# Graph network with attention on one core: the value matrix applied after the weighted sums, and a short last set of chunks

## The chip, the cores and the metric

The kernel runs on one core of one Trainium2 chip. The metric is the device time of one execution in microseconds (us). Engines are named as in the profile: PE (TensorE matmuls), PEld (the loading of matmul weights, which the same engine does), DVE (VectorE), ACT (ScalarE), POOL (GpSimd) and SP (SyncE). POOL and SP have only DMA work and register work in the parts that matter here.

## The reference

There are 6250 nodes with 256 features and 106250 edges, sorted by destination; every node has an edge to itself, so a node has 17 edges in the mean. Two blocks follow each other.

```
h = relu(layernorm(x))
for l in 0, 1, 2:                                    # relational layers, 8 edge types
    msg = (h @ W_rel[l][type])[src]                  # one matrix for each type
    h   = relu(segment_sum(msg, dst) + h @ W_root[l] + bias[l])
x1 = x + h
g  = relu(layernorm(x1))
v  = g @ Wv + bv ;  q = v @ wq + bq ;  k = v @ wk + bk
e  = leaky_relu(q[src] + k[dst], 0.2)
a  = softmax of e over the edges of each dst
out = x1 + segment_sum(a * v[src], dst)
```

## The kernel before, in words

Edges are taken in 831 chunks of 128. Consecutive chunks form sets: 47 sets of 15 chunks and then 9 of 14, 56 in all. A set covers at most 128 consecutive destination nodes, beginning at the destination of its first edge; where the next set begins with the same node, the last chunk of a set is also given to the next one ("ahead"). `node_ranges` gives, for each chunk position in a set, the range of nodes that it can touch. If the input does not fit these ranges, a second, general program runs; it does not run here.

The program has a preparation (edges turned, positions checked, first layernorm, table `tab[0]` written), three layers and the attention phase.

In a layer (`order` loop), each chunk costs one indirect DMA from POOL (L717) that fetches 128 rows of the layer's table, three bf16 parts of each feature row, into `msg` (36 buffers). PE multiplies them (L896) with a 0/1 matrix `hot` that DVE makes (L864) and that separates nodes and edge types. Sums gather in PSUM `bank`s and are copied by ACT to `ag` (`evacuate`, L772). What follows for a set is `finish`, a generator that is advanced by one step after each chunk of the next set: a transposition of the set's own rows (`pt`, L782), 18 f32 matmuls of 256 columns with the weights (L797, L801; each is two PE records) spread over 12 steps, the bias (L805), a split into three bf16 parts and a write to the next table. With its last `yield` that makes 14 steps; the call that finds the generator at its end uses one call more. In the third layer the 18 matmuls take 8 steps, and five steps come after them: residual and write to `xa`, layernorm (L822), two transpositions (L827) with relu (L829), two matmuls with `Wv` (L833), and the bias, the heads q and k (L842) and the write of rows of 257 numbers (v and q) to `hx`. What is left of `finish` after a layer's last chunk runs then. The order of this part is written out by hand (`manual_schedule`), and each engine takes its instructions in that order. SP loads a set's first node and its own rows at chunk 4.

The first gather of a layer reads a table that the layer before has written to its last row.

In the attention phase each chunk is one indirect DMA of 257-number rows of `hx` (48 buffers, `head`). DVE makes a mask (L961), ACT adds q (L968), PE transposes (L970, three PSUM buffers `pq`), ACT and DVE form the logits and their maxima (L973 to L981), ACT takes the exponential of the whole set (L983), PE transposes back (L988, three PSUM buffers `pe`), ACT and DVE copy to `ex` (L991, L993), and PE adds up `ex` times the rows (L995, one f32 matmul of 256 columns for each chunk, two records) into `po`. DVE scales and adds x1 (L1001). Here a planner orders the instructions of each engine when the kernel is built, with program order as priority; each engine takes them in that fixed order.

Of the kernel before, what the change touches and what calls it, by code (L numbers as in the profile page):

```python
# [19 lines left out]
P = 128  # L20
# [6 lines left out]
CW = 15  # L27
SPREAD = 4.5
# [7 lines left out]
def node_ranges(n: int, mean: float) -> list[tuple[int, int]]:  # L36


    wander = math.sqrt(mean - 1.0) / mean**1.5
    out = []  # L40
    for k in range(n):
        a, b = P * k, P * (k + 1) - 1
        lo = math.floor(a / mean - SPREAD * wander * math.sqrt(a) - 1)
        hi = math.ceil(b / mean + SPREAD * wander * math.sqrt(b) + 2)
        out.append((max(lo, 0) if k else 0, min(hi, P) if k < n - 1 else P))
    return out
# [383 lines left out]
def kernel(  # L430
# [28 lines left out]
    NW = -(-NC // CW)  # L459
    NLONG = NC - NW * (CW - 1)  # L460
    NS = NW - NLONG
    CL = NLONG * CW
    sizes = [CW] * NLONG + [CW - 1] * NS
    first_c = [sum(sizes[:t]) for t in range(NW)]
    ranges = {n: node_ranges(n, E / N) for n in (CW, CW - 1)}
# [31 lines left out]
    def by_window(a: bass.AP):  # L497

        return ((slice(0, NLONG), a[:, :CL].rearrange("p (t k) -> p t k", k=CW), CW),
                (slice(NLONG, NW), a[:, CL:NC].rearrange("p (t k) -> p t k", k=CW - 1), CW - 1))  # L500

    with tc.tile_pool(name="prep", bufs=1) as prep, \
# [49 lines left out]
        for at, view, k in by_window(dst_t):  # L552
            nc.vector.tensor_copy(base[:, at], view[0:1, :, 0])
        nc.vector.tensor_copy(front[:, 1:NLONG + 1],
                              dst_t[0:1, CW - 1:CL:CW])
        nc.vector.tensor_copy(front[:, NLONG + 1:NW],
                              dst_t[0:1, CL + CW - 2:NC - (CW - 1):CW - 1])
# [12 lines left out]
        for n in (CW, CW - 1):  # L570
# [19 lines left out]
        for to, of, b in ((loc_p, dst_t, base_b), (seg_p, seg_t, seg_b)):  # L590
            nc.vector.memset(to[:, 0:1], -1.0)
            nc.vector.tensor_tensor(to[:, 1:NLONG + 1], of[:, CW - 1:CL:CW],
                                    b[:, 1:NLONG + 1], ALU.subtract)
            nc.vector.tensor_tensor(to[:, NLONG + 1:NW], of[:, CL + CW - 2:NC - (CW - 1):CW - 1],
                                    b[:, NLONG + 1:NW], ALU.subtract)
# [4 lines left out]
        viol = prep.tile([P, 8], F32)  # L600
# [15 lines left out]


# [10 lines left out]
        nc.vector.tensor_scalar(ends[:, 2:3], base[:, NW - 1:NW], -1.0, float(N - P) - 0.5,  # L628
# [28 lines left out]
    def statistics(pool, xt: bass.AP, n: int):  # L657
        mv = pool.tile([P, 4, 2], F32, name="mv")
        for i in range(n):
            st = pool.tile([P, 6], F32, name="st")  # L660
            nc.vector.bn_stats(st, xt[:, i, :])
            nc.vector.bn_aggr(mv[:, i, :], st)
        rstd = pool.tile([P, 4], F32, name="rstd")
        nc.scalar.activation(rstd[:, :n], mv[:, :n, 1], AF.Sqrt, bias=eps)
        nc.vector.reciprocal(rstd[:, :n], rstd[:, :n])
# [39 lines left out]
    def ordered_path():  # L705
# [7 lines left out]
        k_n = cst.tile([P, NW], F32)  # L713
        bs = path.enter_context(tc.tile_pool(name="bs", bufs=3))
# [14 lines left out]
        with ExitStack() as s:  # L729
# [12 lines left out]
            wv_s = one.tile([P, KH, D], F32)  # L742
            bv_s = one.tile([P, D], F32)
            wq_s = one.tile([P, D], F32)
            wk_s = one.tile([P, D], F32)
            bq_s = one.tile([P, 1], F32)
            bk_s = one.tile([P, 1], F32)
# [14 lines left out]
            def load_head():  # L762
                nc.scalar.dma_start(wv_s, wv.rearrange("(k p) e -> p k e", p=P))
                for to, of in ((bv_s, bv), (wq_s, wq), (wk_s, wk)):
                    nc.scalar.dma_start(to, rows_bcast(of, D))
                for to, of in ((bq_s, bq), (bk_s, bk)):
                    nc.scalar.dma_start(to, rows_bcast(of, 1))

            def evacuate(banks, half: int, ag: bass.AP):

                for h in range(KH):
                    nc.scalar.copy(ag[:, h, :, half * (P // 2):(half + 1) * (P // 2)],  # L772
                                   banks[half][h].rearrange("p (n r) -> p r n", r=R))

            def finish(l: int, at, xt: bass.AP, ag: bass.AP, weights, t: int):


                wr, wo, bb = weights
                pt = ops.tile([P, KH, P], F32, name="pt")
                for k in range(KH):  # L780
                    for i in range(3):
                        nc.tensor.matmul(pt[:, k, :], xt[:, i, k * P:(k + 1) * P], ident_b,  # L782
                                         start=(k == 0 and i == 0), stop=(k == KH - 1 and i == 2),
                                         skip_group_check=True)
                x_t = rp.tile([P, KH, P], F32, name="x_t")
                nc.scalar.copy(x_t, pt)
                yield
                last = l + 1 == L
                parts = STEPS - (6 if last else 2)
# [3 lines left out]
                for i in range(parts):  # L793
                    upto = len(todo) * (i + 1) // parts
                    for r, h in todo[done:upto]:
                        if r < R:
                            nc.tensor.matmul(po, ag[:, h, r, :], wr[:, h, r, :],  # L797
                                             start=(r == 0 and h == 0), stop=False,
                                             skip_group_check=True)
                        else:  # L800
                            nc.tensor.matmul(po, x_t[:, h, :], wo[:, h, :], start=False,  # L801
# [3 lines left out]
                nc.vector.tensor_add(po, po, bb)  # L805
                if not last:
                    hml = rp.tile([P, 3, D], BF16, name="hml")
                    split(hml, po, po, "relu")
                    nc.sync.dma_start(tab[l + 1][ds(at, P), :], hml.rearrange("p s d -> p (s d)"))
                    yield  # L810
                    return
                x0 = rp.tile([P, D], F32, name="x0")
                if t < NW - 1:
                    nc.sync.dma_start(x0, x[ds(at, P), :])
                else:
                    gather(x0, x, last_c)
                x1 = rp.tile([P, 1, D], F32, name="x1")
                nc.vector.scalar_tensor_tensor(x1[:, 0, :], po, 0.0, x0, op0=ALU.max, op1=ALU.add)
                nc.sync.dma_start(xa[ds(at, P), :], x1[:, 0, :])
                yield  # L820
                mv, rstd = statistics(rp, x1, 1)
# [224 lines left out]
```

## Time and profile before

| | us |
|---|---|
| median of three runs (lowest, highest) | 4529.12 (4519.02, 4529.94) |
| the profiled execution | 4520.3 |
| its span, first to last instruction | 4518.4 |
| first gather of layers 1, 2, 3 and of attention | 120.66, 1189.70, 2256.10, 3411.92 |
| last gather of layers 1, 2, 3 and of attention | 1158.45, 2227.32, 3331.59, 4457.52 |

| share of the span | PE | PEld | DVE | ACT | POOL |
|---|---|---|---|---|---|
| busy | 84% | 69% | 45% | 26% | 70% |

A line of a timeline gives start, duration, engine, source line, operation, output and inputs, how many instructions are drawn together, and in brackets how long the engine had been idle and what ended that. A group of instructions gives busy time (overlaps counted once), mean ns of one, and idle time before. A line of the chain of waits gives who waited for whom, the total, how often, and the longest. In a table by stretches the columns are busy us and number of instructions for PE, PEld, DVE, ACT and POOL, then granted PE clock, DMA share and GB/s.

### The profile page before, as it was taken

The numbers are of one execution on the slowest core, as the hardware profiler recorded it, in microseconds if no ns is written. First come the engines' busy times: TensorE is split into PE (matmuls) and PEld (weight loads), VectorE is DVE, ScalarE is ACT, GpSimd is POOL, SyncE is SP. The second block draws the span as 40 slices with busy tenths as digits, with TensorE's granted clock in tenths as the row PEclk, the third lists the DMA queues.
The fourth block names the chain that finished last, engine by engine and source line by source line (L and its number), as shares of the span: only waits on it lengthen the run. The fifth ranks groups of instructions, "written<-read, shape, count | busy, mean of one in ns | idle before, by whom it ended". The sixth has DMA issues, their size and how long they took to land. (4 is left out here: it accounts for less than half of the span.)

```text
span 4518.4 us, 81585 instructions
## 1 busy us (share of the span) xinstructions
PE 3775.3 (84%) x29932; PEld 3129.4 (69%) x29932; DVE 2030.9 (45%) x5907; ACT 1179.9 (26%) x2622; POOL 3177.1 (70%) x3411
## 2 busy tenths in 40 slices
PE   0799999999899999999888989999985777777776
PEld 0677777777677777777677777777774666555555
DVE  6333333333233333333334444444444666666664
ACT  3111111111111111111111111111114555555554
POOL 2777777777577777777577777777636777777773
PEclk5899999999899999999999999999996877778888
DMA  4666666666566666666566666666633444444442
GB/s 152 214 179 180 179 180 179 179 179 181 154 180 180 179 180 180 179 180 180 149 182 186 188 186 186 178 177 179 176 107 96 120 119 119 120 121 120 117 119 60
DMA packets 305210, 722.81 MB, mean 160 GB/s; under 512 B 63179, under 2 KB 158487, under 8 KB 304800
## 3 DMA queue, kind: packets, MB, share of 16 engines
q0 software_dynamic: 199536, 599.93, 47.2%
q1 hardware_dynamic: 94940, 108.40, 7.3%
q10 hardware_dynamic: 10324, 9.18, 0.6%
q8 instruction: 237, 3.88, 0.4%
q14 instruction: 173, 1.42, 0.1%
HBM read 663.43 MB, written 53.87 MB: 159 GB/s over the span
## 5 line engine op out<-in xcount | busy, mean ns | idle before, releaser
L717 POOL DMA_INDIRECT msg<-tab,src_t x2493 | 2357.4, 946 | 855.0 <-issue 398.1
L896 PE MATMUL bank<-hot,msg 128*128 128x104 bf16 (+16 forms) x17982 | 1738.8, 240 | 288.2 <-DMA msg<-tab,src_t 175.1
L896 PEld LDWEIGHTS <-msg 128*128 128x128 bf16 x18972 | 1397.8, 98 | 687.2 <-DMA msg<-tab,src_t 311.2
L797 PE MATMUL po<-wr,ag 128*128 128x256 f32 x5376 | 1494.9, 392 | 6.7 <-DVE hml L655 4.9
L864 DVE TENSOR_SCALAR hot<-up,seg 128x104 bf16<-128x104 f32 (+10 forms) x2493 | 953.0, 430 | 647.4 <-PE bank L896 643.1
L717 POOL DMA_INDIRECT head<-hx,src_t x831 | 785.5, 945 | 306.8 <-issue 138.2
L797 PEld LDWEIGHTS po<-wr,ag 128*128 128x128 f32 x5376 | 898.0, 191 | 66.8 <-DVE hml L655 6.2
L772 ACT COPY ag<-bank 128x512 f32<-128x512 f32 x672 | 361.6, 591 | 1915.7 <-PE bank L896 1903.7
L805 DVE TENSOR_TENSOR po<-po,bb 128x256 f32<-128x256 f32 x168 | 72.6, 432 | 1061.7 <-PE po L801 1026.2
L995 PE MATMUL po<-head,ex 128*128 128x256 f32 x1772 | 451.4, 412 | 1.6 <-DVE ex L993 0.5
L995 PEld LDWEIGHTS po<-head,ex 128*128 128x128 f32 x1772 | 363.8, 211 | 68.0 <-ACT ex L991 14.2
L970 PE MATMUL pq<-ident,qm 128*128 128x128 f32 x886 | 202.0, 320 | 171.1 <-ACT qm L968 169.9
L968 ACT ACTIVATE qm<-other,head 128x128 f32<-128x128 f32 x886 | 299.5, 397 | 146.1 <-issue 117.7
L988 PE MATMUL pe<-ident,c 128*128 128x128 f32 x886 | 190.4, 388 | 134.5 <-ACT c L983 134.5
L974 DVE TENSOR_REDUCE tops<-pq 128x1 f32<-128x512 f32 x224 | 152.4, 680 | 323.4 <-ACT c L973 323.1
L970 PEld LDWEIGHTS pq<-ident,qm 128*128 128x128 f32 x886 | 126.0, 153 | 233.2 <-ACT qm L968 218.7
L988 PEld LDWEIGHTS pe<-ident,c 128*128 128x128 f32 x886 | 162.2, 205 | 154.4 <-ACT c L983 148.7
L961 DVE TENSOR_SCALAR other<-up,loc 128x128 f32<-128x128 f32 x831 | 256.6, 340 | 10.4 <-ACT qm L968 10.4
L801 PE MATMUL po<-wo,x_t 128*128 128x256 f32 x672 | 173.2, 380 | 0.0
L652 ACT ACTIVATE hml<-po 128x256 bf16<-128x256 f32 x112 | 43.0, 384 | 489.1 <-DVE po L805 398.5
L975 DVE SCALAR_TENSOR_TENSOR c<-pq,k_n,c 128x512 f32<-128x512 f32 x224 | 164.7, 735 | 0.0
L991 ACT COPY ex<-pe 128x512 f32<-128x512 f32 x112 | 64.5, 576 | 352.4 <-PE pe L988 352.4
(135 smaller groups left out, 1588.7 us busy)
## 6 DMA issues: line engine op xcount, KB each, us to landing
msg<-tab,src_t POOLq DMA_INDIRECT x2493
xt<-tab SPq DMA_DIRECT2D x168, 192.0 KB
tab<-hml SPq DMA_DIRECT2D x112, 192.0 KB
head<-hx,src_t POOLq DMA_INDIRECT x831
tab<-hml SPq DMA_DIRECT2D x12, 768.0 KB
hx<-row SPq DMA_DIRECT2D x56, 128.5 KB
xa<-x SPq DMA_DIRECT2D x56, 128.0 KB
xt<-xa SPq DMA_DIRECT2D x56, 128.0 KB
```

What stands on the lines that cost most here:

```text
L717: nc.gpsimd.indirect_dma_start(out=to, out_offset=None, in_=table[:N, :], in_offset=bass.IndirectOffsetOnAxis(ap=index, axis=0))
L772: nc.scalar.copy(ag[:, h, :, half * (P // 2):(half + 1) * (P // 2)], banks[half][h].rearrange("p (n r) -> p r n", r=R))
L797: nc.tensor.matmul(po, ag[:, h, r, :], wr[:, h, r, :], start=(r == 0 and h == 0), stop=False, skip_group_check=True)
L801: nc.tensor.matmul(po, x_t[:, h, :], wo[:, h, :], start=False, stop=(h == KH - 1), skip_group_check=True)
L864: nc.vector.tensor_scalar(hot[:, :R * (hi - lo)], up[:, :R * (hi - lo)], seg[:, i:i + 1], None, op0=ALU.is_equal)
L896: nc.tensor.matmul(banks[b][h][:, a - b * SEG // 2:z - b * SEG // 2], w, hot[:, a - lo:z - lo], start=(not begun[b] and s_ == 0), stop=Fal ...
L961: nc.vector.tensor_scalar(other, up[:, :P], refs[j][1], None, op0=ALU.not_equal)
L968: nc.scalar.activation(qm, other, AF.Identity, scale=MASKED, bias=refs[j][0][:, D:HX])
L970: nc.tensor.transpose(pq[:, i, :], qm, ident)
L975: nc.vector.scalar_tensor_tensor(to, flat, k1, to, op0=ALU.add, op1=ALU.max)
L988: nc.tensor.transpose(pe[:, i, :], c_t[:, j * P:(j + 1) * P], ident)
L995: nc.tensor.matmul(po, ex[:, i, :], refs[j][0][:, :D], start=(j == 0), stop=(j == len(refs) - 1))
```

## The change

`Wv` moves to the other side of the weighted sum. Since the weights of a node add up to one, sum(a * (g Wv + bv)) = (sum(a * g)) Wv + bv. So `hx` holds g and q; q and k come from g with the vectors `u` = Wv w and the offsets bv·w + b, which `turn_heads` makes once on the chip, after chunk 7 of layer 3. In attention the weighted sums are formed transposed, in `pf`, with the gathered rows as weights and `ex` as the moving operand: two f32 matmuls of 128 columns for each chunk in place of one of 256. ACT copies `pf` to `fs`, and two f32 matmuls of 256 columns with `Wv` make `po`. `bv` is added to the rows of x1 by DVE. `pe` has two PSUM buffers instead of three.

The sets become 42 of 15 chunks, 14 of 14 and a last one of 5 (57 in all), the last over 64 nodes (`spans`). A call that finds a finished generator goes on to the next one, so no step is lost; in the last set four steps follow each chunk. In that set DVE and ACT share the copies to `ag`. In layer 3 `finish` has 10 steps of matmuls and three after them. SP's loads come at chunk 1, with `x0` among them. The preparation has one more check of the input (three DVE instructions) and one more kind of set.

```diff
-    NW = -(-NC // CW)
...
+    NW = -(-(NC - LAST) // CW) + 1
+    NLONG = NC - LAST - (NW - 1) * (CW - 1)
+    NS = NW - 1 - NLONG
...
+        nc.vector.scalar_tensor_tensor(scr, nxt_r, float(N), dst_r, op0=ALU.min, op1=ALU.subtract)
+        nc.vector.tensor_reduce(viol[:, 8:9], scr, AX.X, ALU.max)
+        nc.vector.tensor_scalar_add(viol[:, 8:9], viol[:, 8:9], -1.5)
...
+            def turn_heads():
+
+                for w, b, u, c in heads:
+                    scr = rp.tile([P, D], F32, name="scr")
+                    col = rp.tile([P, KH], F32, name="col")
+                    diag = rp.tile([P, KH, P], F32, name="x_t")
+                    pt = ops.tile([P, KH, P], F32, name="pt")
+                    for h in range(KH):
+                        nc.vector.scalar_tensor_tensor(
+                            scr, wv_s[:, h, :], 1.0, w, op0=ALU.mult, op1=ALU.mult,
+                            accum_out=col[:, h:h + 1])
+                        nc.vector.tensor_scalar(diag[:, h, :], ident, col[:, h:h + 1], None,
+                                                op0=ALU.mult)
+                        nc.tensor.matmul(pt[:, h, :], ones_p, diag[:, h, :], start=(h == 0),
+                                         stop=(h == KH - 1), skip_group_check=True)
+                    nc.scalar.copy(u, pt.rearrange("p h f -> p (h f)"))
+                    nc.vector.scalar_tensor_tensor(scr, bv_s, 1.0, w, op0=ALU.mult, op1=ALU.mult,
+                                                   accum_out=c)
+                    nc.vector.tensor_add(c, c, b)
...
-                parts = STEPS - (6 if last else 2)
+                parts = STEPS - (4 if last else 2)
...
+                row = rp.tile([P, HX], F32, name="row")
+                nc.scalar.activation(row[:m, :D], x1[:m, 0, :], AF.Relu, bias=shift[:m],
+                                     scale=rstd[:m, 0:1])
+                nc.sync.dma_start(xa[ds(at, m), :], x1[:m, 0, :])
                 yield
-                pt = ops.tile([P, KH, P], F32, name="pt")
-                for k in range(KH):
-                    nc.tensor.transpose(pt[:, k, :], x1[:, 0, k * P:(k + 1) * P], ident)
-                h_t = rp.tile([P, KH, P], F32, name="h_t")
-                nc.scalar.activation(h_t, pt, AF.Relu)
-                yield
-                ph = ops.tile([P, D], F32, name="po")
-                for h in range(KH):
-                    nc.tensor.matmul(ph, h_t[:, h, :], wv_s[:, h, :], start=(h == 0),
-                                     stop=(h == KH - 1))
-                yield
...
+                    final = t == NW - 1
...
-                    if unfinished:
-                        if next(unfinished[0], "done") == "done":
+                    for _ in range(-(-STEPS // (n - 1)) if final else 1):
+                        while unfinished and next(unfinished[0], "done") == "done":
                             unfinished.pop(0)
+                    if l == L - 1 and i == CW // 2:
+                        turn_heads()
-                    if k == 4:
+                    if k == 1:
...
+                        if l == L - 1:
+                            x0 = rp.tile([P, D], F32, name="x0")
+                            if final:
+                                gather(x0, x, last_c)
+                            else:
+                                nc.sync.dma_start(x0, x[ds(at, P), :])
...
+                            nc.vector.tensor_add(xt[:m], xt[:m], bv_s[:m])
...
+                pf = aps.tile([P, KH, P], F32, name="pf")
                 for g, js in enumerate(chunks):
-                    pe = aps.tile([P, 4, P], F32, name="pe", bufs=3)
+                    pe = aps.tile([P, 4, P], F32, name="pe", bufs=2)
...
                     for i, j in enumerate(js):
-                        nc.tensor.matmul(po, ex[:, i, :], refs[j][0][:, :D],
-                                         start=(j == 0), stop=(j == len(refs) - 1))
+                        for h in range(KH):
+                            nc.tensor.matmul(
+                                pf[:, h, :m], refs[j][0][:, h * P:(h + 1) * P], ex[:, i, :m],
+                                start=(j == 0 and h == 0),
+                                stop=(j == len(refs) - 1 and h == KH - 1), skip_group_check=True)
+                fs = rp.tile([P, KH, P], F32, name="fs")
+                nc.scalar.copy(fs[:, :, :m], pf[:, :, :m])
+                po = aps.tile([P, D], F32, name="po")
+                for h in range(KH):
+                    nc.tensor.matmul(po[:m], fs[:, h, :m], wv_s[:, h, :], start=(h == 0),
+                                     stop=(h == KH - 1))
```

## The prediction

> **What bounds the kernel now.** I first read a table of three stretches of 50 us: in the middle of layer 1, late in layer 3, and in attention.
>
> ```profile
> 970.00:1020.00 50.00, 46.02 (x409) 37.28 (x410) 19.08 (x51) 7.24 (x16) 37.81 (x41) 1.00 0.62 181
> 3070.00:3120.00 50.00, 46.21 (x406) 39.84 (x404) 20.47 (x65) 7.14 (x16) 35.84 (x39) 1.00 0.64 183
> 3920.00:3970.00 50.00, 35.27 (x156) 29.20 (x156) 32.37 (x100) 27.59 (x62) 37.82 (x41) 0.76 0.43 120
> ```
>
> POOL shows the same 37.8 us and 40 to 41 gathers in layer 1 and in attention, stages that have little else in common; only in layer 3 it is lower. So next came POOL's own timeline around the ends of the stages.
>
> ```profile
> 1157.20 0.95 POOL L717 DMA_INDIRECT msg<-tab,src_t  x1 [0.30 <-PE bank L896]
> 1158.45 0.95 POOL L717 DMA_INDIRECT msg<-tab,src_t  x1 [0.30 <-issue]
> 1189.70 0.94 POOL L717 DMA_INDIRECT msg<-tab,src_t  x1 [30.31 <-DMA tab<-hml]
> ...
> 2227.32 0.95 POOL L717 DMA_INDIRECT msg<-tab,src_t  x1 [0.30 <-issue]
> 2256.10 0.94 POOL L717 DMA_INDIRECT msg<-tab,src_t  x1 [27.84 <-DMA tab<-hml]
> ...
> 3331.59 0.95 POOL L717 DMA_INDIRECT msg<-tab,src_t  x1 [0.30 <-PE bank L896]
> 3365.24 0.94 POOL L717 DMA_INDIRECT x<-in_x_dram,last_c  x1 [32.71 <-DVE x L818]
> 3411.92 0.94 POOL L717 DMA_INDIRECT head<-hx,src_t  x1 [45.73 <-issue]
> ...
> 4457.52 0.95 POOL L717 DMA_INDIRECT head<-hx,src_t  x1 [0.30 <-issue]
> 4511.10 1.01 POOL L1005 DMA_INDIRECT out_dram<-y,last_i  x1 [52.63 <-POOLq L1010]
> ```
>
> Gathers follow each other every 1.25 us (0.95 and a gap of 0.30 whatever is named as its cause). 830 such steps are 1037.6 us: exactly the gather stretch of layers 1 and 2 (1037.8 and 1037.6). Layer 3 takes 1075.5, attention 1045.6. So the span is 120.7 before the first gather, 4 x 1037.6, and what POOL loses: 31.3 and 28.8 between layers, 37.9 inside layer 3, 80.3 before attention, 8 inside it, 60.9 after its last gather. An edit is worth what it takes from these losses, and no more.
>
> Why layer 3 is slow, from the chain of waits:
>
> ```profile
> PE pt L827 <- DVE x L822: 112.1, 56, 3.3
> ```
>
> PE stands 2.0 us in each set, in its fixed order, for the layernorm inside `finish`. I work out PE's own load from its record spacing: a bf16 record of 240 columns starts every 0.10 us, an f32 record of 256 columns every 0.216; over the node ranges that makes 8.2 us of sums and 8.3 us of `finish` in a set of 15, 16.5 against the gathers' 18.75. Layer 3 adds four records at 0.216, two transpositions at 0.11 and the 2.0: 19.6, over 18.75. PE falls behind until all 36 buffers are full, so that 36 x 1.25 = 45 us of work stand behind the last gather; hence the 80.
>
> In attention the exponentials show the rate, and PE's order in one set the reason.
>
> ```profile
> 3807.05 1.99 ACT L983 ACTIVATE c<-c,sm 128x2048 f32<-128x2048 f32 x1
> ...
> 3865.07 1.99 ACT L983 ACTIVATE c<-c,sm 128x2048 f32<-128x2048 f32 x1
> ```
>
> ```profile
> 3809.18 2.82 PE L988 MATMUL pe<-ident,c 128*128 128x128 f32 x12 [2.38 <-ACT c L983]
> 3811.79 0.63 PE L970 MATMUL pq<-ident,qm 128*128 128x128 f32 x2
> 3812.22 6.24 PE L995 MATMUL po<-head,ex 128*128 128x256 f32 x24
> 3818.30 0.60 PE L988 MATMUL pe<-ident,c 128*128 128x128 f32 x4
> 3818.74 0.82 PE L970 MATMUL pq<-ident,qm 128*128 128x128 f32 x6
> 3819.58 1.99 PE L995 MATMUL po<-head,ex 128*128 128x256 f32 x8
> ```
>
> Between these two are three sets: 58.02 / 3 = 19.34 us each, 0.6 more than the gathers need. It is a ring, not a full engine: PE's sums hold back the next set's transpositions, then DVE and ACT form logits and exponential while PE stands (waits on L968 and L983 are 123.5 and 110.1 us in the 900 us from 3500, 5 us a set). The compute falls behind, ends up 48 heads late, and so 60.9 us follow the last gather.
>
> **The change part by part**, against the profiled span of 4518.4 us.
>
> Preparation: an int subtraction (1.09), a reduction (1.08), 0.13 for the check, and about eight more small DVE instructions at 0.15 for the third kind of set. DVE runs without a break up to the check's result, and everything waits for that: **+3.5**.
>
> Layers 1 and 2, their ends. Before, from the last gather: 5.2 until PE ends the last chunk; 5.2 for 24 records left of the set before (the nine sets of 14 lose a step each); 2.3 because `po` has one buffer; 9.7 for 36 records, partly at a low clock; 2.2 for bias and split; 6.6 for the write: 31.2. After: no steps are left over, but the set of five holds 10.7 us of PE work (8.3 of `finish`, 2.4 of sums) in 6.25 us of gathers, so PE ends 4.4 later, at 9.6; then 0.8 for the copies, 36 x 0.216 = 7.8, 2.3 and 6.6: 27.1. Gain 4.1, the same for layer 2: **-8.2**. The write has half the rows; at nothing gained, at most 3. Steps earlier in the sets cost nothing: a set of 14 then needs 15.9 of PE against 17.5.
>
> Layer 3: PE loses the two transpositions, four records and the 2.0 wait, and gets nothing back in `finish`: DVE loses two instructions of 0.43 and gains a small one, ACT keeps one of 0.38 and loses two. 16.5 is under 18.75, so POOL's pace returns: 1037.6 and 1.25 for `x0`'s gather, **-36.6**. `turn_heads` stops PE once for some 5 us (DVE: 4 x (0.5 + 0.34)); 36 buffers and a slack of 2.3 a set cover it. Without that slack it would cost 5. On SP's queue `x0`, `xa` and `hx` come in a new order; the next set's load at chunk 1 stands behind the `hx` write of the set before, and is needed only 14 chunks later.
>
> Before attention: 9.6, 0.8 and 7.8 as above, then the tail as at 3400.4 to 3408.7 without transpositions and `Wv`: bias, x1, statistics 2.3, shift 0.3, relu 0.8, q 0.6, issue 0.2; and 3.2 until `hx` is written: 25.6 in place of 80.3, **-54.7**.
>
> Attention, matmuls: 64 records of 128 columns for 32 of 256. Transpositions of 128 columns, each with its own weights, start every 0.11 at full clock (six against four above: 0.22 for two), 256 columns every 0.216: 7.0 against 6.9. But these are no transpositions; the nearest row of an f32 load of the other kind lasts 191 ns (L797). I take 0.11, since loads begin while the matmul before them runs, and keep 0.19 for the rivals.
> Then four records with `Wv` (0.86 at full, 1.7 at half clock), behind a copy on ACT of 0.39. They end a set, where PE stands 5 us: taken at 0, at most 2.1 with the copy's latency. `pe` with two buffers puts half of the next set's transpositions between the sums of one set, where before all came after 24 records: it may win up to 1.9 (the 8 records after them) or lose an `ex` copy of 0.69; taken at 0. DVE's `bv` addition, 0.43 (L805), I count in full, because DVE runs without a break from L974 to L981 in the ring: 57 x 0.43 = **+24.5**; it could be 0, or more where it stands for `xt`'s load. One set more: 5 sets lose a chunk (0.6 each), a short ring of about 11 comes in, and the last set ends about 5 sooner: **+3**.
>
> Sum: 4518.4 + 3.5 - 8.2 - 36.6 - 54.7 + 24.5 + 3 = 4449.9; the profiled execution took 1.9 more than its span, so 4452. That execution lies 9 us (0.2%) under the median of the runs shown, near the lowest; I do not correct for it.
>
> **The rivals.** *Attention reaches POOL's pace.* If the new order shortens the ring by 0.6, compute keeps up; after the last gather come about 30 us (13 for the set of 14, 6 for the short one, 11 for `Wv`, the store and the end) in place of 60.9. Against 1106.5 from the first gather that is 1041 + 32: 33 less, with neither +24.5 nor +3: 4391. For it speaks the clock: the transpositions above start every 0.21 after the pause and every 0.11 later, some 2.5 us lost in each set, and `Wv`'s records would shorten that pause.
> The Trainium skill has this as a rule (TensorE: Matmul & The Clock Gate, Part 1: The HAM clock gate): the array runs at half clock until it has been busy for a window of about 3.4 us, and falls back after an idle one. The trace agrees, 0.21 against 0.11.
>
> *The added work lies on the ring*: `Wv`'s 0.86 beside the 0.43, 57 x 1.29 = 74: 4427 + 74 = 4501; with the copy, 2.1 a set, 4547.
>
> *Weight loads are not hidden.* At 0.19 for each of 64 records the sums take 12.2 for 6.9: 57 x 5.3 = 300, about 4727, slower. It decides from (93 + 6.9 x 57) / (57 x 64) = 0.133 us a record, 93 being the gain without the 24.5. Against it: transpositions reload for every record and keep 0.11. For it: the two-record f32 load is a longer row.
> The Trainium skill speaks for it (TensorE: Matmul & The Clock Gate, Back-to-back issue gap): a stream of loads and matmuls of 128 columns takes about 81 ns each where the matmul alone needs 56; by that ratio (an estimate from the page) a record takes 0.16, 3.2 more a set, and the time is about 4610. The trace does not show that: six bf16 loads of 128 columns (L782) take 0.37 in all, under 0.07 each.
>
> *Layer 3 stays behind POOL*, because something else in its fixed order stops PE: 37 and most of the 45 of lag return, about 4525.
>
> **How the numbers follow.** Forecast 0.45 (4427 to 4480 as the addition and the order cost 0 to 0.9), POOL's pace 0.25, work on the ring 0.15, loads 0.12, layer 3 unchanged 0.03. About 0.3% is what a measurement of this kernel can tell from no change. Faster: the first two and nearly all of the third, 0.84; same 0.03; slower 0.13. The range goes from a little under the second case to the upper part of the third, 4383 to 4520.
>
> **What would show it.** POOL in layer 3 at 40 gathers in 50 us throughout; about 26 us from its last gather to the first of attention; 27 and 24.7 after layers 1 and 2; no wait of PE on the layernorm; PE records of `pf` every 0.11 at full clock; three exponentials of long sets within 56 to 61 us. The prediction is wrong if that ring grows by more than 1.7 us a set, or if the records of `pf` take more than 0.133.

## The result, and the profile after

The changed kernel took 4408.88 us (median of four runs, 4404.90 to 4410.09) against 4529.24 for the kernel before beside it: a ratio of 0.9738, with a 95% interval of 0.9721 to 0.9755. The profiled execution took 4404.90, with a span of 4403.0. That is 43 us under the forecast of 4452, inside its range, and 18 from the time of the rival "attention reaches POOL's pace" (4391).

The three stretches of 50 us of the table before, in the changed kernel (its stages begin earlier):

```profile
970.00:1020.00 50.00, 46.63 (x417) 39.44 (x418) 19.34 (x53) 7.88 (x18) 37.82 (x41) 1.00 0.64 182
3070.00:3120.00 50.00, 47.26 (x425) 39.59 (x424) 23.86 (x81) 9.61 (x21) 37.82 (x41) 1.00 0.69 194
3820.00:3870.00 50.00, 38.92 (x277) 35.52 (x278) 33.98 (x97) 29.18 (x67) 37.81 (x41) 0.86 0.45 122
```

POOL (the fifth pair) now has 41 gathers in layer 3 too, where it had 39. Its timeline around the ends of the stages, at the same places as before:

```profile
1160.47 0.95 POOL L730 DMA_INDIRECT msg<-tab,src_t  x1 [0.30 <-issue]
1194.99 0.94 POOL L730 DMA_INDIRECT msg<-tab,src_t  x1 [33.57 <-DMA tab<-hml]
...
2232.41 0.95 POOL L730 DMA_INDIRECT msg<-tab,src_t  x1 [0.30 <-PE bank L924]
2264.05 0.94 POOL L730 DMA_INDIRECT msg<-tab,src_t  x1 [30.70 <-DMA tab<-hml]
...
3305.69 0.95 POOL L730 DMA_INDIRECT msg<-tab,src_t  x1 [0.30 <-issue]
3333.14 0.94 POOL L730 DMA_INDIRECT head<-hx,src_t  x1 [26.50 <-issue]
...
4371.83 0.94 POOL L730 DMA_INDIRECT head<-hx,src_t  x1 [0.30 <-ACT qm L1008]
```

Differences of starts give the account, which adds up to the spans' difference of 115.4:

| part | before | after | change | forecast |
|---|---|---|---|---|
| before the first gather | 120.7 | 122.7 | +2.0 | +3.5 |
| pauses after layers 1 and 2 | 60.0 | 66.2 | +6.1 | -8.2 |
| gathers of layers 1 and 2 | 2075.4 | 2075.2 | -0.2 | 0 |
| gathers of layer 3 | 1075.5 | 1041.6 | -33.9 | -36.6 |
| pause before attention | 80.3 | 27.5 | -52.9 | -54.7 |
| attention to the end | 1106.5 | 1069.9 | -36.6 | +27.5 |

Two rows have the wrong sign: the ends of layers 1 and 2, and attention.

For attention, the wait of ACT that tells who sets the pace, from the waits between 3400 and 4300 us, in total, times and longest; below it the same wait between 3500 and 4400 us of the kernel before:

```profile
ACT qm L1008 <- DMA head<-hx,src_t: 143.9, 169, 2.8
...
ACT qm L968 <- DMA head<-hx,src_t: 0.2, 1, 0.2
```

ACT now waits for gathered rows to land. POOL sets the pace again, 1038.7 us for 830 steps, and 31.2 follow the last gather in place of 60.9. Three exponentials of long sets are 56.7 us apart in the mean, where they were 58.0. PE's order in one set, from the timeline, against the 12 transpositions and 24 records in a row before:

```profile
3779.95 1.09 PE L1029 MATMUL pe<-ident,c 128*128 128x128 f32 x8 [0.82 <-ACT c L1023]
...
3782.04 3.74 PE L1038 MATMUL pf<-ex,head 128*128 128x128 f32 x32
3785.61 0.93 PE L1029 MATMUL pe<-ident,c 128*128 128x128 f32 x7
...
3786.92 3.80 PE L1038 MATMUL pf<-ex,head 128*128 128x128 f32 x32
```

32 records of `pf` take 3.74 us, about 0.11 each: loads and matmuls overlap, as the sum assumed. Over the whole phase 83% of the spacings between `pf` records are 0.11 us and 15% are 0.21, the two values that the prediction read from the transpositions after a pause and later; the mean is 0.128. The rule on streams of loads and matmuls in the Trainium skill (TensorE: Matmul & The Clock Gate, Back-to-back issue gap), from which I had estimated 0.16, does not show here.

For the pauses, PE's timeline at the end of layer 1, where the last gather starts at 1160.47:

```profile
1163.54 0.43 PE L924 MATMUL bank<-hot,msg 128*128 128x104 bf16 x6
...
1165.90 1.99 PE L837 MATMUL po<-wr,ag 128*128 128x256 f32 x8 [1.59 <-DVE hml L666]
...
1168.13 2.80 PE L837 MATMUL po<-wr,ag 128*128 128x256 f32 x12
...
1175.18 1.00 PE L924 MATMUL bank<-hot,msg 128*128 128x328 bf16 x6
...
1177.76 7.20 PE L837 MATMUL po<-wr,ag 128*64 128x256 f32 x32 [1.30 <-ACT ag L812]
```

The five chunks of the last set (104, 152, 168, 176 and 328 columns) do not follow each other; `finish` of the set before stands between them, and PE first waits for `po`, which DVE's split still reads. PE ends the last chunk 15.7 us after the last gather, not 9.6. The same wait runs through all sets of 14:

```profile
PE po L837 <- DVE hml L666: 17.2, 14, 1.6
...
PE po L797 <- DVE hml L655: 2.7, 2, 2.0
```

The first line is the changed kernel from 900 to 1177 us, 1.2 us in each of 14 cases; the second is the kernel before in the same stretch.

### The profile page after: what moved, and what is told of

Same layout as the page of the kernel before. It is cut to its first block, busy times and chain, and to the rows that moved or that the text cites. A ratio compares the mean times of both kernels' runs of the same rounds, so it can differ in the third digit from the quotient of the medians.

```text
span 4403.0 us, 85522 instructions
## 1 busy us (share of the span) xinstructions
PE 3739.3 (85%) x31754; PEld 3152.4 (72%) x31754; DVE 2040.9 (46%) x5977; ACT 1198.5 (27%) x2643; POOL 3180.0 (72%) x3421
## 5 line engine op out<-in xcount | busy, mean ns | idle before, releaser
L924 PE MATMUL bank<-hot,msg 128*128 128x104 bf16 (+17 forms) x17982 | 1746.3, 240 | 322.7 <-DMA msg<-tab,src_t 208.7
L837 PE MATMUL po<-wr,ag 128*128 128x256 f32 (+1 forms) x5472 | 1537.5, 393 | 45.0 <-DVE hml L666 34.0
L892 DVE TENSOR_SCALAR hot<-up,seg 128x104 bf16<-128x104 f32 (+12 forms) x2493 | 954.7, 430 | 738.1 <-PE bank L924 730.8
L837 PEld LDWEIGHTS po<-wr,ag 128*128 128x128 f32 (+1 forms) x5472 | 903.7, 190 | 114.1 <-DVE hml L666 39.3
L1038 PE MATMUL pf<-ex,head 128*128 128x128 f32 (+1 forms) x3548 | 470.1, 296 | 1.4 <-DVE ex L1035 1.2
L1038 PEld LDWEIGHTS pf<-ex,head 128*128 128x128 f32 x3548 | 460.0, 213 | 9.2 <-DVE ex L1035 3.2
L1008 ACT ACTIVATE qm<-other,head 128x128 f32<-128x128 f32 (+1 forms) x887 | 321.4, 398 | 296.2 <-DMA head<-hx,src_t 184.0
L1010 PE MATMUL pq<-ident,qm 128*128 128x128 f32 (+1 forms) x887 | 182.2, 303 | 123.2 <-ACT qm L1008 118.9
L841 PE MATMUL po<-wo,x_t 128*128 128x256 f32 (+1 forms) x684 | 176.4, 380 | 0.0
L1015 DVE SCALAR_TENSOR_TENSOR c<-pq,k_n,c 128x512 f32<-128x512 f32 (+1 forms) x226 | 165.5, 732 | 0.0
```

The costliest lines, as they stand in the source:

```text
L837: nc.tensor.matmul(po[:m], ag[:, h, r, :m], wr[:, h, r, :], start=(r == 0 and h == 0), stop=False, skip_group_check=True)
L841: nc.tensor.matmul(po[:m], x_t[:, h, :m], wo[:, h, :], start=False, stop=(h == KH - 1), skip_group_check=True)
L892: nc.vector.tensor_scalar(hot[:, :R * (hi - lo)], up[:, :R * (hi - lo)], seg[:, i:i + 1], None, op0=ALU.is_equal)
L924: nc.tensor.matmul(banks[b][h][:, a - b * SEG // 2:z - b * SEG // 2], w, hot[:, a - lo:z - lo], start=(not begun[b] and s_ == 0), stop=Fal ...
L1008: nc.scalar.activation(qm[:, :m], other[:, :m], AF.Identity, scale=MASKED, bias=refs[j][0][:, D:HX])
L1010: nc.tensor.transpose(pq[:m, i, :], qm[:, :m], ident)
```

## The experiments

Four runs were made on a chip where the kernel before took 4523.82 us, and the control on one where it took 4525.51. The other seven ran on three chips where it took 5723, 5860 and 5869 us and the gathers of all three layers and of attention took longer in every kernel; these are compared with the kernel before and the runs of the same chip only.

**One size: a last set of 14.**

```diff
-LAST = 5
+LAST = 14
```

> The changed kernel with a last set of 14 chunks instead of 5: the sets are again 47 of 15 and 9 of 14, everything else stays new (value matrix after the sums, no step lost). Theory: the short set costs time at the ends of layers 1 and 2, because its 8.3 us of finish do not fit beside 6.25 us of gathers; without it PE ends the last chunk some 10 us after the last gather and not 15.7, so the two pauses fall from 34.5 and 31.6 to about 29 and 26 and the pause before attention by as much, while the stretch after attention's last gather grows from 31.2 to about 40: in all about 4403, within 10 us of the changed kernel. Rival: the short set is worth time at the layers' ends, and the pauses were long for another reason: then they stay at 34 and 31 or grow, and the time is 4420 or more.

4387.91 us (4382.94 to 4391.41), ratio to before 0.9697 (0.9681 to 0.9713). The pauses are 25.2, 23.2 and 20.6 against 34.5, 31.6 and 27.5, and attention to the end is 1072.8. PE's timeline at the end of layer 1, where the last gather starts at 1162.26:

```profile
1165.62 4.71 PE L924 MATMUL bank<-hot,msg 128*128 128x160 bf16 x60
1170.17 0.50 PE L822 MATMUL pt<-ident_b,xt 128*128 128x128 bf16 x6
1170.58 7.28 PE L837 MATMUL po<-wr,ag 128*128 128x256 f32 x32
```

PE ends the last chunk 8.1 us after the last gather and goes straight on. The short set costs some 9 us at each of two ends of layers and 7 before attention, 25 in all, and wins at most 3 in attention. The theory had the sign, but too little of it: the pauses fell further than it said, and what follows attention's last gather is 32.2 us and not 40, so the gain is 21 us and not 6. All the rest of the change kept, this is the fastest kernel of the study.

**The wait for `po` taken away.** The bias is added into an SBUF tile, so `po` is free after one DVE instruction.

```diff
-                nc.vector.tensor_add(po[:m], po[:m], bb[:m])
+                pb = rp.tile([P, D], F32, name="pb")
+                nc.vector.tensor_add(pb[:m], po[:m], bb[:m])
...
-                    split(hml[:m], po[:m], po[:m], "relu")
+                    split(hml[:m], pb[:m], pb[:m], "relu")
...
```

> The changed kernel, with the bias addition of finish writing to SBUF, so that the PSUM buffer po is free after that one instruction (0.43 us) and not after the whole split (2.2 us). Theory: in sets of 14 PE waits 1.2 us in every set for po's only buffer, is therefore behind POOL when the short set begins (first chunk 7.9 us after its gather instead of 3.4), and this makes the pauses of 34.5 and 31.6 longer than the forecast 27.1; with the wait gone PE starts the short set 4 to 5 us earlier, both pauses fall by 5 to 6 us and the time to about 4396. Rival: PE's lag in the sets of 14 is plain work; then the pauses fall by the 1.6 us of the last wait at most, and the time stays within 4 us of 4409.

4405.81 us, ratio 0.9741 (0.9725 to 0.9758). The wait on the split is gone from the sets of 14, PE ends the last chunk of layer 1 at 10.6 us after the last gather (15.7 before this edit), and the pauses are 29.6 and 27.3: 4.9 and 4.3 shorter. So the wait for `po` makes up about half of what the last set of five costs at an end of a layer. The time did not show the gain of 9: it lies in the range of the rival (within 4 us of 4409). The gathers of layers 1 and 2 took 2.3 us more each, that of layer 3 3.2 more, and the pause before attention 1.5 more. The trace shows where the gathers lost it. In layers 1 and 2, 28 of them last 1.00 to 1.20 us in place of 0.95, 4.2 us in all, and each of the 28 overlaps the subtraction L666 on DVE, which in this run reads two SBUF tiles. For example:

```profile
166.15 0.42 DVE L666 TENSOR_TENSOR hml<-pb,hml 128x256 bf16<-128x256 f32 x1 [0.47 <-ACT hml L665]
...
166.26 1.14 POOL L730 DMA_INDIRECT msg<-tab,src_t  x1 [0.30 <-issue]
```

Leaving out the first gather of the layer, no gather of layers 1 and 2 is that long in any other run; in the changed kernel L666 reads `po`, in PSUM. In layer 3 there are 30 such gathers (4.6 us) against 13 (1.8). So the edit takes PE's wait away and loses most of what it won on POOL, the engine that sets the pace. The control below has gathers in layers 1 and 2 that are longer by 1.6 and 1.7, but spread evenly over all steps and without one such gather.

**PE's wait in layer 3, in the kernel before.** One more step between the layernorm and the transpositions, one step less for the 18 matmuls.

```diff
-                parts = STEPS - (6 if last else 2)
+                parts = STEPS - (7 if last else 2)
...
                 yield
+                yield
                 pt = ops.tile([P, KH, P], F32, name="pt")
```

> The kernel before with one thing changed: in layer 3 one more step is put between the layernorm and the two transpositions, and the 18 matmuls take 7 steps instead of 8. All the work stays, PE has only no longer to wait for DVE at that place. Theory: of the 3.1 us that PE had above the sums and the matmuls in each set of layer 3, 2.0 were this wait; without it the load is 17.6 against 18.75 of gathers, POOL's pace returns (layer 3 takes 1037.6 instead of 1075.5) and the lag of 45 us behind the last gather goes to under 10: some 65 to 75 us less, 4455 to 4465. Rival: the matmuls and transpositions with Wv are what holds layer 3, and the wait only fills what would be idle anyway: then no more than 15 us less.

4504.80 us, ratio 0.9956 (0.9939 to 0.9973). That is 19 us less, a little over the rival's 15 and far under the theory's 65 to 75. Layer 3 takes 1061.2 in place of 1075.5, the pause before attention is still 79.2. PE's wait ahead of the transpositions, between 2270 and 3310 us:

```profile
PE pt L828 <- DVE hot_p L861: 71.8, 46, 2.5
...
PE pt L828 <- DVE x L822: 6.5, 5, 2.8
```

It is 78.3 in 51 cases, 1.5 a set in place of 2.0 (99.6 in 51 in the kernel before): the edit took away only a quarter of the wait that it was made to remove. By the prediction's sum PE then has 19.1 us a set against 18.75, still more than POOL, and it is still behind at the layer's end. An excess of 0.85 a set gave 37.9 us over the layer; one of 0.35 gives 23.6. So the sum is not exact, but its statement holds that the pause stays as long as PE is over POOL's pace at all.

**Layer 3 without the work.** In the kernel before, the transpositions and the matmuls with `Wv` are left out; g goes to `hx`, and the heads are taken from it without `Wv`. This leaves out the value matrix and its bias altogether.

```diff
-                parts = STEPS - (6 if last else 2)
+                parts = STEPS - (4 if last else 2)
...
+                row = rp.tile([P, HX], F32, name="row")
+                nc.scalar.activation(row[:, :D], x1[:, 0, :], AF.Relu)
                 yield
-                pt = ops.tile([P, KH, P], F32, name="pt")
-                for k in range(KH):
-                    nc.tensor.transpose(pt[:, k, :], x1[:, 0, k * P:(k + 1) * P], ident)
-                h_t = rp.tile([P, KH, P], F32, name="h_t")
-                nc.scalar.activation(h_t, pt, AF.Relu)
-                yield
-                ph = ops.tile([P, D], F32, name="po")
-                for h in range(KH):
-                    nc.tensor.matmul(ph, h_t[:, h, :], wv_s[:, h, :], start=(h == 0),
-                                     stop=(h == KH - 1))
-                yield
-                nc.vector.tensor_add(ph, ph, bv_s)
-                row = rp.tile([P, HX], F32, name="row")
-                nc.scalar.copy(row[:, :D], ph)
...
```

> The kernel before, with the third layer's transpositions and the two matmuls with Wv left out of finish and its other 18 matmuls spread over ten steps; the rows written to hx hold g and the heads are taken from g itself, so the output is not the reference's. Theory (PE's load of 19.6 us a set in layer 3, wait included, makes the third layer slow): 16.5 us a set is less than POOL's 18.75, so layer 3's gathers take 1037.6 to 1041 us in place of 1075.5 and the pause before attention falls from 80 to 33 to 40 us: 75 to 85 us less in all, about 4440 to 4450, ratio 0.981 to 0.984. Rival (the earlier trial with one step more won only 19 us, so something else in PE's order holds layer 3 too): layer 3 stays over 1050 us, 20 to 45 less in all, ratio 0.990 to 0.996.

> The kernel before with the third layer's transpositions and matmuls with Wv left out (the output is not the reference's), once more for the same reason. Theory: layer 3's gathers take 1037.6 to 1046 us in place of 1075.5, the pause before attention 33 to 42 us in place of 80, 70 to 85 us less in all, ratio 0.981 to 0.985. Rival (something else in PE's order holds layer 3): layer 3 over 1050 us, 20 to 45 less in all, ratio 0.990 to 0.996.

Both runs were on chips where the kernel before was long: 5656.27 against 5723.23, ratio 0.9869 (0.9845 to 0.9892), and 5776.10 against 5860.03, ratio 0.985 (0.9827 to 0.9872). That is 67 and 84 us less, near and in the theory's 70 to 85 and outside the rival's 20 to 45. The stages say it more plainly. On the first of these chips the gathers of layers 1, 2 and 3 took 1234.6, 1235.9 and 1243.4 us; in a run with layer 3 as before (the next experiment, same chip) they took 1240.6, 1238.0 and 1298.1. Layer 3's excess over layer 1, 57.6, falls to 8.8 (on the second chip it is 6.3 in this run). The removed work with its wait is therefore most of the reason, 49 of 58 us, why layer 3 was longer than layer 1 there. The pause before attention fell there from 73.8 to 60.1 only, not to the theory's 33 to 42: on these chips the pauses after layers 1 and 2 are over 60 as well.

**No step lost, alone, in the kernel before.**

```diff
-                        if next(unfinished[0], "done") == "done":
+                        while unfinished and next(unfinished[0], "done") == "done":
                             unfinished.pop(0)
```

> The kernel before, where alone a call that finds a finished generator goes on to the next one, so no step is lost. Theory (5.2 us of each layer's end were 24 records left of the set before): the pauses after layers 1 and 2 fall from 31.3 and 28.8 to about 25 and 23, as in the changed kernel with a last set of 14, and the pause before attention by 3 to 6: 13 to 18 us less, ratio 0.996 to 0.997. Rival (steps earlier in the sets of 14 make PE's load there higher, and the records return as lag): the pauses fall by less than 3 each, total within 5 us, ratio 0.999 to 1.001.

5722.07 us against 5723.23, ratio 0.9996 (0.9984 to 1.0008): nothing. On that chip the pauses after layers 1 and 2 are 66.7 and 64.4 us, and records taken earlier did not shorten the time, as the rival had it. Whether it helps where POOL sets the pace was not measured.

**Two buffers for `pe`, alone, in the kernel before.** This is the one edit of attention that the prediction took at nothing.

```diff
-                    pe = aps.tile([P, 4, P], F32, name="pe", bufs=3)
+                    pe = aps.tile([P, 4, P], F32, name="pe", bufs=2)
```

> The kernel before with two PSUM buffers pe instead of three in attention, nothing else. Theory (order): the planner then puts the next set's transpositions between the sums of one set, and this is what took attention to POOL's pace; three exponentials come in 56.3 us instead of 58.0, the stretch after the last gather falls from 60.9 to about 40, the time by about 20 to 4509. Rival (form): the pace came from the sums in two matmuls of 128 columns and the work behind them; two buffers alone then make the ring longer by up to 0.7 us (an ex copy), and the time rises by 0 to 40 us.

4486.78 us, ratio 0.9921 (0.9904 to 0.9937). The gathers of attention take 1037.5, and 31.5 us follow the last one (the theory said about 40): 1069.0 for the whole phase, against 1106.5 before and 1069.9 in the changed kernel. The time is 37 us less; the theory had said 20. PE's order in a set and ACT's wait (3500 to 4400 us) show the same two things as in the changed kernel, without its sums, `Wv` or `bv`:

```profile
3803.05 1.97 PE L988 MATMUL pe<-ident,c 128*128 128x128 f32 x8 [2.80 <-ACT c L983]
...
3805.45 3.84 PE L995 MATMUL po<-head,ex 128*128 128x256 f32 x16
3809.12 1.04 PE L988 MATMUL pe<-ident,c 128*128 128x128 f32 x8
...
3811.13 3.72 PE L995 MATMUL po<-head,ex 128*128 128x256 f32 x16 [0.54 <-DVE ex L993]
```

```profile
ACT qm L968 <- DMA head<-hx,src_t: 189.8, 254, 2.3
```

With two buffers the third block of transpositions back must wait for a copy, and the planner puts transpositions `pq` of the next set and half of the sums ahead of it. DVE and ACT get the next set's logits while PE is still busy with the sums. The order of DVE and ACT is another one too; the edit changes nothing else.

**The opposite edit: three buffers for `pe` in the changed kernel** and two for `pq` in place of three, which is a second change.

```diff
-                    pe = aps.tile([P, 4, P], F32, name="pe", bufs=2)
+                    pe = aps.tile([P, 4, P], F32, name="pe", bufs=3)
...
-                    pq = aps.tile([P, 4, P], F32, name="pq", bufs=3)
+                    pq = aps.tile([P, 4, P], F32, name="pq", bufs=2)
```

> The changed kernel with three PSUM buffers for the transpositions back (pe) in attention, as before, and two for pq, so that PSUM holds them; sums and Wv in the new form. Theory (the order that two buffers force brought attention to POOL's pace): attention falls back, three sets take 57.5 to 59 us between exponentials, its gathers 1042 to 1060 us and what follows the last one 50 to 65 us: 25 to 45 us more than the changed kernel, 4434 to 4454, ratio to before 0.980 to 0.985. Rival (the new form of the sums brought it): gathers 1038 to 1040, 31 to 34 after the last, within 6 us of the changed kernel's time, ratio 0.973 to 0.976.

> The changed kernel with three PSUM buffers for pe and two for pq, once more: the chip of the run before was one on which the kernel before itself took 5723 us, and there the question of POOL's pace in attention does not arise. Theory (the order that two buffers for pe force brought attention to POOL's pace): from the first gather of attention to the last 1042 to 1060 us and 50 to 65 us after it, 25 to 45 us more than the changed kernel's 4409 in all, ratio to before 0.979 to 0.985. Rival (the new form of the sums brought it): 1038 to 1040 and 31 to 34, ratio 0.972 to 0.976.

> The changed kernel with three PSUM buffers for pe and two for pq, a third time, in the hope of a chip on which the kernel before takes 4520 to 4530 us. There, by the theory (the order that two buffers for pe force brought attention to POOL's pace): 1042 to 1060 us from the first gather of attention to the last and 50 to 65 us after it, ratio to before 0.979 to 0.985. By the rival (the new form of the sums brought it): 1038 to 1040 and 31 to 34, ratio 0.972 to 0.976. Where the kernel before takes over 5000 us, neither is tested.

5702.16 against 5723.23 (0.9955, 0.9937 to 0.9972), 5767.22 against 5860.03 (0.9842, 0.9825 to 0.9858) and 5769.91 against 5868.67 (0.9837, 0.9819 to 0.9854): three times on a chip of the long kind, where neither side of the question is tested. (Attention took 1646 us on the first of these chips, where two runs with attention as before took 1620 and 1635; on the second it took 1662 against 1700.) What stands without a time is the order laid down when this kernel is built: in 55 of 57 sets PE has again 12 or 13 transpositions back and then 48 records of sums in a row. That it would fall back by 25 to 45 us at POOL's pace remains a conclusion.

**`bv` left out as well.** The kernel with three buffers, and the rows of x1 do not get `bv`, so the output lacks it.

```diff
-                            nc.vector.tensor_add(xt[:m], xt[:m], bv_s[:m])
```

> As the run with three buffers for pe, and bv is not added to the rows of x1, so the output lacks bv. It asks what DVE's addition costs where compute and not POOL sets attention's pace. Theory of the prediction (DVE runs without a break in the ring, each addition costs its 0.43): 57 x 0.43 = 24.5 us less than the run with the addition. Rival (the addition falls into DVE's own waits): within 5 us of it. If the run with three buffers is at POOL's pace after all, the two agree and this tells nothing.

5816.66 us, ratio to before 1.0159 (1.0135 to 1.0182), on the chip of the first of the three runs above: 114 us *more* than with the addition. From the first gather of attention to the end it takes 1764 us, the other 1646. Neither theory allowed this. With 57 instructions fewer the planner lays down another order on PE, DVE and ACT, though PE's 12 transpositions and 48 records in a row are there in both. Two runs on this chip with one and the same attention code differ by 14 us in that phase, so 118 is far more than that. The order is the likely cause, but no run shows it. The price of the addition itself stays open.

**The control: the changed kernel once more.**

> The changed kernel itself, unaltered, as the control for the runs with three PSUM buffers for pe. Where the kernel before takes over 5700 us: by the theory (two buffers give PE the better order, whatever sets the pace) attention, from its first gather to the end, is more than 20 us shorter than the 1662 to 1664 us of the last two runs with three buffers, and the ratio to before under 0.980. By the rival (the order matters only within 1% of POOL's pace) attention stays within 15 us of that and the ratio between 0.981 and 0.987. Where the kernel before takes 4520 to 4530 us: 4409 again, ratio 0.972 to 0.975, and nothing new.

It came to a chip with 4525.51 for the kernel before: 4416.88 (4414.49 to 4418.21), ratio 0.9759 (0.9743 to 0.9775). The pauses are 35.1, 30.7 and 29.1, attention to the end 1074.2, layer 3 1045.5. That is a little outside the 0.972 to 0.975 that was expected. The signs of the account are the same but for the gathers of layers 1 and 2, which are 3 us longer here, and its rows are good to about 4 us from chip to chip, 12 us in the span.

## Why the prediction was right or wrong

*Preparation*, +3.5: +2.0. Right in kind, a little too dear.

*Ends of layers 1 and 2*, -8.2: +6.1. The step that failed is "the set of five holds 10.7 us of PE work ... so PE ends 4.4 later, at 9.6". PE ended at 15.7. It took the set's first chunk 7.9 us after its gather, where 9.6 implies 3.9, and then needed 12.8 us for 10.7, 1.6 of it a wait for `po`. I had noticed that `po` has one buffer, but counted its 2.3 only at the very end; with no step lost, `finish` of one set follows directly on that of the other in every set of 14, and the wait comes each time. The experiment with `pb` shows that the wait was 5 of the 6 us: there PE ends at 10.6. And I compared the short set with the old end of the layer, not with a long last set without lost steps, so I did not see that it costs 9 us. The rest of the change gives about 6 there (31.3 to 25.2 in the run with a last set of 14); that this is the steps no longer lost was not shown, since that edit alone ran only on a chip of the long kind.

*Layer 3*, -36.6: -33.9 here, -30 in the control. The reasoning held: PE's load of 19.6 against 18.75 with three causes. The run without the work shows, on another chip, that most of the excess lies in these lines; the trial with one step more removed too little of the wait to price wait and work apart. PE now waits for rows to land in layer 3 (67.1 us in all, `bank` on `msg`, 2270 to 3310; 1.9 before), which says that it is ahead of POOL. Of the 4.0 us that the layer still takes above POOL's pace, 2.3 come at `x0`'s gather, where the sum had 1.25, and 1.8 in 13 gathers of over 1.00 us, all while DVE forms the heads from `row` (L869).

*Before attention*, -54.7: -52.9. Right within 2 us, though a term was off: PE ended the last chunk 9.0 us after the last gather (forecast 9.6), but all but two of the 36 records after it start only 3.8 us later and not 0.8, because the copies to `ag` wait on ACT and DVE behind the relu and the heads of the set before.

*Attention*, +27.5: -36.6, the largest error. The step that failed is "`pe` with two buffers ...: it may win up to 1.9 ... or lose an `ex` copy of 0.69; taken at 0". The upper bound was the right one to look at: 0.6 a set is enough to bring compute to POOL's pace. After that the `bv` addition (+24.5) and the extra set (+3) hardly show: the phase takes 1069.9 us with them and 1069.0 in the run with two buffers alone, and ACT has waits to spare. A cost counted in full on a ring that is 0.6 us over another bound was a choice between two regimes; the sum treated it as a straight line. The rival was given with 0.25, and its estimate of 1041 + 32 is the measured 1038.7 + 31.2. Its condition, a ring shorter by 0.6 through the new order, is what came; but its price was left at nothing in the sum, and what I argued for it was the clock. That rose to 0.88 as a mean over 3400 to 4300 us, from 0.80. With two buffers alone it is 0.83 and the pace is reached as well, though in the set shown the eight transpositions after ACT's exponential still take 1.97 us, about 0.21 apart. So the order that two buffers bring is enough by itself in the kernel before, and the gain of the clock is not what makes the difference there. That the changed kernel would miss POOL's pace without it was not shown.

*The rivals.* `Wv` on the ring and weight loads that are not hidden did not occur: two `Wv` matmuls take 1.13 us (four records) behind a wait of 1.08, within PE's idle time, and records of `pf` start every 0.11.

Against the profiled execution of 4404.9 the forecast of 4452 was too high by 64 in attention and too low by 14 at the ends of layers and by 3 in the other rows together.

## What to carry to other kernels

Where a ring is a few per cent over another bound, price an edit by whether it takes the ring under that bound, and look first at edits that only change the order on the engine everyone waits for: one buffer *fewer* was worth 37 us in the kernel before, with nothing else changed in attention. A short last tile saves a tail only if its work still fits into its shorter time with what is left of the tile before it; compare it with a full last tile. Before costing a pipelined step that now follows directly on its predecessor, look for a tile with one buffer between them. And when an edit frees one engine by moving a tile from PSUM to SBUF, look at the engine that sets the pace as well.

## What the runs showed of the hardware that was not expected

A gather that overlaps a DVE instruction with two SBUF operands can take longer. In layers 1 and 2 of the run with `pb`, L666 runs 108 times beside the gathers, and 28 gathers that overlap it last 1.00 to 1.20 us in place of 0.95. In the changed kernel L666 runs as often with one operand in PSUM, and no gather there is lengthened. Not every overlap costs something, and which moment of the gather matters was not tested.

On three chips the kernel before took 5713 to 5874 us, 26 to 30% more than the median shown at first, in all runs. The median durations of the costliest instructions were the same (a gather occupies POOL for 0.95 us there too); what differed is when an instruction started. In the run with no step lost, from the timeline of attention:

```profile
4738.94 0.85 PE L970 MATMUL pq<-ident,qm 128*128 128x128 f32 x2 [1.48 <-ACT qm L968]
...
4742.99 0.69 ACT L973 ACTIVATE c<-pq,sm 128x512 f32<-128x512 f32 x1 [3.72 <-remote]
```

ACT needs the first of the two transpositions, which ends at 4739.42 in the trace, and starts 3.6 us after that; at the same place in the kernel before, on the chip of its profile, it starts 0.04 us after it (at 3806.46). In this run POOL stops 57 times in attention for over 1.5 us, about once in each set, 9.4 us in the mean; in the kernel before it does so three times, at most 2.5 us. The traces of these chips also hold only 4.1 to 4.7 records of landings for each gather, where the others hold about 15.9, and well under half as many records of semaphore updates, so what a wait in them is put down to is weak evidence. What lies behind this, the runs do not say. It changes which edit pays: the steps no longer lost were worth nothing there.
